# Two projection loads between an exchange's copies, four output stores from GpSimd to SyncE, and two broadcast loads behind an exchange, in a fused cross-attention block

## The chip, the core and the metric

The kernel runs on one core of one Trainium2 chip. The metric is device time in microseconds (us); the kernel before the change has a median of 761.75 us over three runs (761.52 to 764.06).

A core has five engines, each with a queue of its own that is worked off in order: TensorE (PE in the profile, with PEld for its weight loads), VectorE (DVE), ScalarE (ACT), GpSimd (POOL) and SyncE (SP), which here only issues DMA transfers. Engines wait for each other through semaphores. An SPq row of the profile is SP's queue at a transfer's issue, not the transfer itself.

## What is computed

One cross-attention block over 4 batches, 512 queries and 512 keys, width 512, 16 heads of 32, float32 throughout. The mask is all true.

```python
x = layer_norm(hidden, ln1_w, ln1_b)
q = x @ q_w + q_b
k = enc @ k_w + k_b
v = enc @ v_w + v_b                            # each split into 16 heads of 32
attn = softmax(where(mask, q @ k.T / sqrt(32), lowest))
hidden = (attn @ v) @ cproj_w + cproj_b + hidden
y = gelu(layer_norm(hidden, ln2_w, ln2_b) @ fc_w + fc_b)   # 512 -> 2048
out = hidden + y @ proj_w + proj_b                         # 2048 -> 512
```

## The kernel before

**Blocks.** Attention is cut into 32 blocks, numbered p = 0 to 31. Block p treats batch p // 8, a group of four heads (w = p // 2, so four groups a batch) and half of the queries (half = p % 2). `block` (L349) computes eight tiles of scores on PE (L329); VectorE adds the mask and takes the minimum (L335), ScalarE exponentiates (L339), and VectorE transposes the probabilities in 32 x 32 squares into a buffer `tb` (L347, L372), of which there are two, used in turn. PSUM tiles for scores and products come from two rings of four, used in order (`acc_tile`).

**The exchange.** The transposed squares must then move between the four groups of 32 partitions. `copies` (L397) does it: four GpSimd copies stay within a group (L405), and twelve DMA copies on SP of 136 KB each (L410) go from one group to another, in three rounds d = 1, 2, 3 of four. The target is a tile `pT`, or for some blocks a part of the big buffers `gt` and `xe`. `attend(w, half)` (L413), the product of probabilities and values (L427), reads the whole target some blocks later: in the order written out near the end, block p begins with `attend` of block p - 2 from p = 10 on, and of p - 3 from 3 to 8.

**The order of work.** There is no scheduler. `put(p, ...)` lists for each block the work that fills PE between its scores and its end: preparation of later heads' q, k, v, the output product of the attention, and of the MLP a pair of `fc` blocks (`fc_by_pair`, PE L668) or parts of the projection (`proj`, L774 and L755). `fill(0)` and `fill(1)` run items up to a cost of `CHAIN`, the exchange is issued after `fill(1)`, and `fill(2)` runs what is left. A cost of 0.0 lets an item run within the same `fill`; `next_` gives 0.01, so that an item behind a full `fill(1)` goes to `fill(2)`, behind the exchange.

**MLP weights.** Eight slots in `pbt` take turns (`load_mlp`, L604): a load of 256 KB is issued from SP, in the order of `weights`, as soon as in the program's order the last use of its slot has been issued. Batch 0's projection works on blocks of sums and differences in place, so its slots are also read by late adds on GpSimd (`join`, L622), which block 29 pops from `S["late"]`. Block 29 does the last part of batch 0's projection and the `fc` pair 2 of batch 1; block 30 does pair 3 and the first product of batch 1's projection (`proj_whole`, L755), which reads the four weights 2, 3, 0, 1 in that order. Weights 2 and 3 are loaded in block 28's wake, 0 and 1 by `load_mlp` after block 29's exchange, with two more behind them.

**Batch 0's result** (`hid4`) is complete after those late adds. `store_out(0)` (L828) writes it with four DMA stores of 256 KB, issued from GpSimd at L830. Block 30 then loads two tiles of batch 1 into the same buffer (`load_hid`, L555), which waits for the stores of those tiles, and GpSimd adds a row to them (L438).

**Batch 1's first normalisation.** Its row factors are stored to DRAM and read back, broadcast to 128 partitions, by two loads of 256 KB into `hid2` (`load_rn`, L216). GpSimd multiplies and adds them to the four transposed input tiles `raw` (`ln1_rows`, L221, four operations in block 2 and four in block 3), and ScalarE applies weight and bias (`ln1_affine`, L225, block 4). In block 1 the loads are issued together with batch 1's encoder input (`load_enc`, 1 MB), ahead of that block's exchange.

After block 31, the rest of the MLP runs in larger pieces (`last_mlps`, L668, L901 and others).

Of the kernel before, what the change touches and what calls it, by code (L numbers as in the profile page):

```python
# [20 lines left out]
P = 128  # L21
# [32 lines left out]
def xattn_block(ctx: ExitStack, tc: tile.TileContext, x, rawT, encT, mask, q_w, k_w, v_w, c_w, fc_w, p_w, vecs, rows, out):  # L54
    nc = tc.nc
# [40 lines left out]
    def k_q(w, i):  # L96
        n = w % 4 * 2 + i
        return pbt[:, n * D : (n + 1) * D]

    def mlp_w(n):  # L100
        return pbt[:, (n + MW) * D : (n + MW + 1) * D]
# [16 lines left out]
    S = {"gelu": [], "late": []}  # L118
    count = [0, 0, 0, 0, 0, 0]
    Q = [nc.sync]  # L120

    def acc_tile(name):
        n = count[5]
        count[5] += len(banks) > 1
        return banks[n // 4 % len(banks)].tile([P, D], F32, tag="acc", name=name)
# [51 lines left out]
    def queue(b):  # L177
        return Q[0] if b else nc.sync

    def load_enc(b):  # L180
        for d in range(ND):
            queue(b).dma_start(out=eT[:, d, :], in_=encT[b, ts(d, P), :])
# [17 lines left out]
    def load_raw(b):  # L200
        S["xn", b] = [tiles.tile([P, L], F32, tag="xn", name=f"raw_{b}_{d}") for d in range(ND)]
        for d in range(ND):
            nc.sync.dma_start(out=S["xn", b][d], in_=rawT[b, ts(d, P), :])

    def store_rn(b):
        nc.vector.transpose(rnT, rn)
        d = S["rn", b] = dram.tile([2, L], F32, tag=f"rn{b}", name=f"rn{b}")
        for i in range(NI):
            nc.sync.dma_start(
                out=d.rearrange("a (t i q) -> i (a t) q", i=NI, q=HD)[i], in_=rnT[i * HD : i * HD + 2 * NT, :]  # L210
            )

    def load_rn(b):
        S["rows", b] = [hid2[:, i] for i in range(2)]
        for i in range(2):
            nc.sync.dma_start(out=S["rows", b][i], in_=S["rn", b][i : i + 1, :].broadcast_to([P, L]))  # L216

    def ln1_rows(b, *ds):
        for d in ds:
            for i, op in enumerate((ALU.mult, ALU.add)):  # L220
                nc.gpsimd.tensor_tensor(S["xn", b][d], S["xn", b][d], S["rows", b][i], op)  # L221
# [21 lines left out]
    def load_w(w, queue=None, names=("wk", "wq", "wv")):  # L243

        if w >= NW:
            return
        g = w % NG
        for i, (n, src) in enumerate((("wk", k_w), ("wq", q_w), ("wv", v_w))):
            if n in names:
                S[n, w] = kqv_w(w, i)  # L250
                (queue or Q[0]).dma_start(out=S[n, w], in_=src[:, g, :, :])

    def next_w(w, name):
        if w != SINGLE - 1:
            load_w(w + (2 if w < SINGLE else 1), names=(name,))
# [11 lines left out]
    def prep_q(w):  # L267
        b, g = divmod(w, NG)
        qT = k_q(w, 1)
        parts = [slice(0, L)] if w else [slice(0, 2 * P), slice(2 * P, L)]  # L270
        for c in parts:
            acc = acc_tile(f"accq_{w}_{c.start}")[:, c]
            for d in range(ND):
                nc.tensor.matmul(acc, S["wq", w][:, d, :], xT[:, d, c], start=(d == 0), stop=(d == ND - 1))  # L274
            nc.scalar.activation(qT[:, c], acc, AF.Identity, bias=qb[:, g : g + 1], scale=-scale)
        next_w(w, "wq")
        S["qT", w] = qT

    def prep_v(w):
        b = w // NG  # L280
        v = five.tile([P, NT, P], F32, tag="v", name=f"v_{w}")
        acc = acc_tile(f"accv_{w}")
        for t in range(NT):
            for d in range(ND):
                nc.tensor.matmul(  # L285
                    acc[:, ts(t, P)], eT[:, d, ts(t, P)], S["wv", w][:, d, :],
                    start=(d == 0), stop=(d == ND - 1),
                )
        load_w(w + 2, names=("wv",))
        nc.scalar.copy(v, acc.rearrange("p (t f) -> p t f", t=NT))  # L290
        S["v", w] = v
        if w:
            v_bias(w)
# [25 lines left out]
    def v_bias(w):  # L319
        v, bias = S["v", w], row[:, 2, ts(w % NG, P)]  # L320
        nc.gpsimd.tensor_tensor(v, v, bias[:, None, :].broadcast_to([P, NT, P]), ALU.add)  # L321
# [59 lines left out]
            exchange()  # L381
        fill(2)

    waiting, held = [], {}

    def target(w, half):
        pair = 2 * w + half
        return "gt" if pair in IN_G else "xe" if pair in IN_XE else "pT"
# [8 lines left out]
    def copies(w, half):  # L397
        tb, to = S["tb", w, half], target(w, half)
        if to == "pT":
            pT = one.tile([P, NI, PW + 2 * HD], F32, tag="pT", name=f"pT_{w}_{half}")  # L400
        else:
            pT = (gt if to == "gt" else xe).rearrange("p (i n) -> p i n", i=NI)

        for i in range(NI):
            nc.gpsimd.tensor_copy(pT[ts(i, HD), i], tb[ts(i, HD), i])  # L405
        for d in range(1, NI):
            for i in (0, 2, 1, 3):
                j = (i + d) % NI

                nc.sync.dma_start(out=pT[ts(j, HD), i], in_=tb[ts(i, HD), j])  # L410
        S["pT", w, half] = pT

    def attend(w, half):  # L413
# [175 lines left out]
    for name, b, i, *_ in products:  # L589
# [6 lines left out]
    weights = [(*k, n, i % MW) for i, (k, n) in enumerate(last_use.items())]  # L596
# [3 lines left out]
    free = [  # L600
        next((o[3] for o in reversed(weights[:i]) if o[4] == w[4]), -1) for i, w in enumerate(weights)
    ]

    def load_mlp():  # L604

        while count[0] < len(weights) and free[count[0]] < count[1]:
            name, b, f, _, n = weights[count[0]]
            w = mlp_w(n)
            if name == "fc":
                w = w.rearrange("p (d f) -> p d f", d=ND)  # L610
            Q[0].dma_start(out=w, in_=fc_w[:, f, :, :] if name == "fc" else p_w[ts(f, P), :])
            S[name + "w", b, f] = w if name == "fc" else n + MW
            count[0] += 1
# [10 lines left out]
    def a_sums(a11, a12, a21, a22, s1, s2, s3, s4, engine=None):  # L624
        add(engine or nc.vector, s1, a21, a22)
        sub(s3, a11, a21, engine)
        sub(s2, s1, a11, engine)
        sub(s4, a12, s2, engine)
# [69 lines left out]
    def raw_pair(b, c):  # L698
        return [S["fcw", b, 2 * c + i] for i in range(2)]

    def fc_sums(ahead=2):

        while count[3] < len(fc_pairs) and count[3] < count[4] + ahead:
            b, c = fc_pairs[count[3]]
            if ("fcw", b, 2 * c + 1) not in S:
                return
            x, y = raw_pair(b, c)
            s = wsum[:, count[3] % 2]
            a_sums(x[:, :2], x[:, 2:], y[:, :2], y[:, 2:], s[:, 0], s[:, 1], y[:, :2], s[:, 2], nc.gpsimd)
            if b == 0:  # L710
                nc.gpsimd.dma_start(out=sums_dram[c, :, :3], in_=s)
                nc.gpsimd.dma_start(out=sums_dram[c, :, 3], in_=y[:, :2])
            S["ws", b, c] = s[:, 0], s[:, 1], y[:, :2], s[:, 2]
            count[3] += 1
# [48 lines left out]
    def proj(b, q, part):  # L763
# [61 lines left out]
        if (q, part) != (NQ - 1, 2):  # L825
            load_mlp()

    def store_out(b):  # L828
        for t in range(NT):
            nc.gpsimd.dma_start(out=out[b, ts(t, P), :], in_=S["hid", b, t])  # L830

    wa = [gt[:, i * 2048 : i * 2048 + 1024].rearrange("p (i d f) -> p i d f", i=2, d=ND) for i in range(2)]
    ws = [gt[:, i * 2048 + 1024 : i * 2048 + 2048].rearrange("p (i k f) -> p i k f", i=4, k=2) for i in range(2)]
# [264 lines left out]
    CHAIN, TURN = 3.4, 0.5  # L1098

    def do(fn):  # L1100
        return [(0.0, fn)]

    def next_(fn):
        return [(0.01, fn)]

    def A(w):
        if w >= NW:
            return []
        return [
            (CHAIN, lambda: prep_k(w)),  # L1110
            (CHAIN, lambda: prep_q(w)),
            (CHAIN, lambda: prep_v(w)),
        ]
# [69 lines left out]
    def some(n):  # L1183
        taken = []
        while n > 0:
            n -= 1 if mlp[0][0] == CHAIN else 2
            taken.append(mlp.pop(0))
        assert n == 0
        return taken
# [4 lines left out]
    def hid_(b, *ts_):  # L1194
        return do(lambda: load_hid(b, ts_))
# [21 lines left out]
    def put(p, *work, before=(), mid=()):  # L1217

        work = [item for part in work for item in part]
        ahead[p], mids[p] = list(before), list(mid)  # L1220
        fills[p] = work

    k2, q2, v2 = A(2)
    k3, q3, v3 = A(3)
# [1 line left out]
    k5, q5, v5 = A(5)  # L1226
    k6, q6, v6 = A(6)
    put(0, [(CHAIN, lambda: prep_v(1)), v2], do(lambda: (load_raw(1), store_rn(1))), [k2])
    put(1, [k3, (0.0, lambda: prep_q(1)), (CHAIN, lambda: (prep_v(3), load_enc(1), load_rn(1)))])
    put(2, [q2], [q3], do(lambda: ln1_rows(1, 0, 1)))  # L1230
    put(3, [k4], do(lambda: ln1_rows(1, 2, 3)), [v4])
    put(4, [k5, v5], do(lambda: ln1_affine(1)))
# [39 lines left out]
    put(26, c[3:], do(lambda: attend(12, 0)), pre(0, 3, "w"), some(1))  # L1272
    put(27, some(3))
    put(28, some(3))
    put(29, some(1), do(lambda: (fc_sums(), S["late"].pop()())), some(2), do(lambda: (load_mlp(), store_out(0))))
    put(30, some(3), mid=hid_(1, 2, 3))
    put(31, some(3))

# [2 lines left out]
    for p in range(2 * NW):  # L1281
        w, half = divmod(p, 2)
# [81 lines left out]
```

## Time and profile before

| what | value |
|---|---|
| median of three runs | 761.75 us (761.52 to 764.06) |
| the profiled execution's own time | 762.13 us |
| its span, from the first to the last instruction | 760.4 us |
| mean granted PE clock over the span | 0.997 |
| DMA, mean over the span | 177 GB/s |
| SP's transfers (queue q1) | 126.73 MB |
| GpSimd's transfers (queue q0) | 7.01 MB |

A row of a timeline gives start and length in us, engine, line, operation, and output and input by their names; behind it stands in brackets how long the engine was idle before, and for whom it waited. A row of the chain gives start, length and who held the end at that time. In a table of stages the busy time of each engine is followed by the granted PE clock, the busy share of the 16 DMA engines and GB/s. Lines are those of the kernel before; behind the change they are two or three higher.

### The profile page before, as it was taken

How to read it: one execution, taken by the hardware profiler on the slowest of the kernel's cores; microseconds unless marked ns; L12 is line 12 of the kernel's file. 1: busy time of each engine (PE TensorE's matmuls, PEld its weight loads, DVE VectorE, ACT ScalarE, POOL GpSimd, SP SyncE). 2: the span in 40 equal slices, each digit the busy share in tenths (PEclk: the TensorE clock that was granted, in tenths of full speed). 3: DMA queues.
4: the chain of work that ended last, by engine and by line, in shares of the span. 5: the costliest groups of instructions: out<-in, count | busy, mean ns of one | idle time of the engine just before them, and what ended most of it. 6: DMA issues, size and time to landing. Idle time of an engine off the chain costs nothing.

```text
span 760.4 us, 13322 instructions
## 1 busy us (share of the span) xinstructions
PE 751.2 (99%) x4514; PEld 535.9 (70%) x4514; DVE 618.2 (81%) x1229; ACT 341.0 (45%) x776; POOL 405.6 (53%) x405
## 2 busy tenths in 40 slices
PE   8999999999999999999999999999999999999998
PEld 6655555467667546576655775458888889988998
DVE  3888999879988779877988998848877986957765
ACT  2566776555874575648843577401202221021200
POOL 1539448368687987667869975532050005403153
PEclk9999999999999999999999999999999999999999
DMA  9999888466796797666747758667824512046001
GB/s 324 341 248 245 208 215 251 107 191 185 212 253 208 199 267 188 166 187 165 196 117 213 178 144 250 152 203 236 270 98 134 156 37 91 29 139 220 2 15 43
DMA packets 60580, 134.62 MB, mean 177 GB/s; under 512 B 11312, under 2 KB 17072, under 8 KB 60384
## 3 DMA queue, kind: packets, MB, share of 16 engines
q1 hardware_dynamic: 58448, 126.73, 59.0%
q0 software_dynamic: 1920, 7.01, 2.8%
q8 instruction: 36, 0.59, 0.3%
q14 instruction: 32, 0.26, 0.1%
q10 hardware_dynamic: 144, 0.02, 0.0%
HBM read 69.23 MB, written 11.02 MB: 106 GB/s over the span
## 4 chain that ended last, share of the span: by engine, by line
PE 93%; DMA 2%; POOL 2%; DVE 1%; SPq 1%; issue 0%; DVEq 0%; POOLq 0%
PE q L668 23%; PE r L901 10%; PE sc L329 8%; PE av L427 7%; PE acck L262 7%; PE accq L274 7%; PE accc L469 6%; PE accv L285 5%; PE accp L755 4%; PE accv L310 3%; PE q1p L962 2%; PE tp L169 1%; SPq L410 1%; PE q1j L774 1%; PE q2j L774 1%; PE q7j L774 1%
## 5 line engine op out<-in xcount | busy, mean ns | idle before, releaser
L339 ACT ACTIVATE ptt<-ptt,mn 128x512 f32<-128x512 f32 x256 | 181.7, 711 | 146.9 <-DVE mn L335 146.9
L335 DVE CUSTOM_DVE_ANT_0 ptt<-sc,mb 128x512 f32<-128x512 f32 x256 | 160.6, 682 | 19.5 <-PE sc L329 19.5
L347 DVE STREAM_TRANSPOSE tb<-ptt 128x1024 f32<-128x1024 f32 x128 | 153.3, 1217 | 1.5 <-ACT ptt L339 1.5
L405 POOL COPY pT<-tb 32x1088 f32<-32x1088 f32 x96 | 104.6, 1089 | 34.7 <-DVE oT L432 11.8
L668 PE MATMUL q<-yT,gt 128*128 128x256 f32 x320 | 78.9, 379 | 0.0
L689 ACT ACTIVATE ga<-ga,vec 128x512 f32<-128x512 f32 x40 | 26.7, 714 | 93.3 <-DVE ga L622 83.6
L329 PE MATMUL sc<-pbt 32*128 32x512 f32 x512 | 67.1, 615 | 0.0
L668 PEld LDWEIGHTS q<-yT,gt 128*128 128x128 f32 x320 | 60.7, 190 | 8.2
L668 PE MATMUL q<-ys,gt 128*128 128x256 f32 x240 | 61.6, 379 | 0.0
L262 PE MATMUL acck<-xe,ptt 128*128 128x512 f32 x128 | 58.7, 601 | 0.0
L274 PE MATMUL accq<-xe,ptt 128*128 128x512 f32 (+1 forms) x136 | 58.1, 573 | 0.0
L668 PEld LDWEIGHTS q<-ys,gt 128*128 128x128 f32 x240 | 45.6, 190 | 6.2
L622 DVE TENSOR_TENSOR ga<-q,ga 128x512 f32<-128x512 f32 (+1 forms) x60 | 36.2, 603 | 15.6 <-PE q L668 12.6
L427 PE MATMUL av<-pT,v 128*32 128x256 f32 x768 | 46.4, 382 | 1.9 <-POOL gt L619 1.9
L339 ACT ACTIVATION_READ_ACCUMULATOR ptt<-ptt,mn 128x1 f32 x256 | 47.8, 187 | 0.0
L274 PEld LDWEIGHTS accq<-xe,ptt 128*128 128x128 f32 x136 | 25.0, 190 | 30.4 <-issue 23.0
L438 POOL TENSOR_TENSOR hid<-hid,row 128x512 f32<-128x512 f32 x18 | 23.9, 1356 | 41.6 <-DMA hid<-xa 41.6
L329 PEld LDWEIGHTS sc<-pbt 32*128 32x128 f32 x512 | 27.7, 183 | 26.0 <-issue 17.5
L262 PEld LDWEIGHTS acck<-xe,ptt 128*128 128x128 f32 x128 | 23.0, 190 | 31.4 <-issue 21.5
L469 PE MATMUL accc<-wc,oT 128*128 128x512 f32 x96 | 42.5, 597 | 0.0
L321 POOL TENSOR_TENSOR v<-v,row 128x512 f32<-128x512 f32 x16 | 20.3, 1278 | 40.6 <-ACT v L290 29.8
L285 PEld LDWEIGHTS accv<-ptt,xe 128*128 128x128 f32 x320 | 36.9, 192 | 5.8 <-DVE mn L335 2.5
(264 smaller groups left out, 1440.8 us busy)
## 6 DMA issues: line engine op xcount, KB each, us to landing
pT<-tb SPq DMA_DIRECT2D x288, 136.0 KB
pbt<-p_w_dram SPq DMA_DIRECT2D x40, 256.0 KB
gt<-ws SPq DMA_DIRECT2D x20, 512.0 KB
gt<-tb SPq DMA_DIRECT2D x48, 136.0 KB
xe<-tb SPq DMA_DIRECT2D x48, 136.0 KB
pbt<-fc_w_dram SPq DMA_DIRECT2D x24, 256.0 KB
gt<-fc_w_dram SPq DMA_DIRECT2D x20, 256.0 KB
ptt<-k_w_dram SPq DMA_DIRECT2D x16, 256.0 KB
```

The costliest lines, as they stand in the source:

```text
L262: nc.tensor.matmul(acc, S["wk", w][:, d, :], eT[:, d, :], start=(d == 0), stop=(d == ND - 1))
L274: nc.tensor.matmul(acc, S["wq", w][:, d, :], xT[:, d, c], start=(d == 0), stop=(d == ND - 1))
L285: nc.tensor.matmul(acc[:, ts(t, P)], eT[:, d, ts(t, P)], S["wv", w][:, d, :], start=(d == 0), stop=(d == ND - 1),)
L329: nc.tensor.matmul(S["sc", w, qt][h], qT[r, ts(qt, P)], kT[r, :], start=True, stop=True)
L335: nc.vector.tensor_tensor_reduce(out=s, in0=S["sc", w, qt][h], in1=S["mb", w // NG], scale=1.0, scalar=FMAX, op0=ALU.add, op1=ALU.min, acc ...
L339: nc.scalar.activation(s, s, AF.Exp, bias=mn, scale=-1.0, accum_out=S["sums", w][:, qt, h : h + 1])
L347: nc.vector.transpose(tv[:, qt % 2, 2 * k : 2 * k + 2], S["ps", w, qt, k])
L405: nc.gpsimd.tensor_copy(pT[ts(i, HD), i], tb[ts(i, HD), i])
L427: nc.tensor.matmul(av[ts(h, HD), : 2 * P].rearrange(shape, **kw), v[:, t, ts(h, HD)], p[t][h], start=(t == 0), stop=(t == NT - 1),)
L469: nc.tensor.matmul(acc, S["oT", b][:, g, ts(t, P)], wc[:, g, :], start=(g == 0), stop=(g == NG - 1))
L668: nc.tensor.matmul(o, x[:, k], y[:, k], start=(k == 0), stop=(k == 1))
L901: nc.tensor.matmul(r, x[:, c], w[:, c], start=(c == 0), stop=(c == NP // 2 - 1))
```

## The change

Three edits:

1. The first two of the four projection loads that followed block 29's exchange (weights 0 and 1) are issued on SP between that exchange's first round of four copies and the other eight. `copies` gets a hook for it (`between`), and `load_mlp` a limit on the number of loads. The other two loads stay behind.
2. Batch 0's four output stores are issued by SP, behind block 29's exchange and ahead of the remaining two loads; before, GpSimd issued them, and the loads stood ahead in the program.
3. The two broadcast loads of batch 1's row factors go from ahead of block 1's exchange to behind it, still on SP.

On SP the order around block 29 is, before: 12 copies, 4 projection loads, 2 reloads of `hid`, 2 projection loads. After: 4 copies, 2 projection loads, 8 copies, 4 stores, 2 projection loads, 2 reloads, 2 projection loads. The first moved load waits for the second of GpSimd's late adds. PE's, VectorE's and ScalarE's instructions and their order are the same; GpSimd loses its four stores.

```diff
-    waiting, held = [], {}
+    waiting, held, between = [], {}, {}
...
                 nc.sync.dma_start(out=pT[ts(j, HD), i], in_=tb[ts(i, HD), j])
+            if d == 1:
+                between.pop((w, half), lambda: None)()
...
-    def load_mlp():
+    def load_mlp(most=len(weights)):
 
-        while count[0] < len(weights) and free[count[0]] < count[1]:
+        end = min(count[0] + most, len(weights))
+        while count[0] < end and free[count[0]] < count[1]:
...
     def store_out(b):
         for t in range(NT):
-            nc.gpsimd.dma_start(out=out[b, ts(t, P), :], in_=S["hid", b, t])
+            nc.sync.dma_start(out=out[b, ts(t, P), :], in_=S["hid", b, t])
...
-    put(1, [k3, (0.0, lambda: prep_q(1)), (CHAIN, lambda: (prep_v(3), load_enc(1), load_rn(1)))])
+    put(1, [k3, (0.0, lambda: prep_q(1)), (CHAIN, lambda: (prep_v(3), load_enc(1)))], next_(lambda: load_rn(1)))
...
-    put(29, some(1), do(lambda: (fc_sums(), S["late"].pop()())), some(2), do(lambda: (load_mlp(), store_out(0))))
+    put(29, some(1), do(lambda: (fc_sums(), S["late"].pop()())), some(2), do(lambda: (store_out(0), load_mlp())))
+    between[14, 1] = lambda: load_mlp(2)
```

## Prediction

> **What bounds the kernel now.** I read the page's busy times first, then TensorE's waits, then the timeline of the one long wait that this change can reach.
>
> ```profile
> PE 751.2 (99%) x4514; PEld 535.9 (70%) x4514; DVE 618.2 (81%) x1229; ACT 341.0 (45%) x776; POOL 405.6 (53%) x405
> ```
>
> ```profile
> PE av L427 <- POOL gt L619: 1.9, 1, 1.9
> PE accp L755 <- DMA pbt<-p_w_dram: 1.7, 1, 1.7
> ```
>
> TensorE (PE) is busy for 99% of the span. No matmul is added or removed, so the change can only win where PE stands still or runs slowly, and lose by making PE wait anew. Two waits over a microsecond remain inside the work; the second, at L755 for a projection load, is the one that the moved loads end.
>
> ```profile
> 467.15 1.88 PE L755 MATMUL accp<-pbt,gt 128*128 128x512 f32 x4
> 470.75 3.01 PE L755 MATMUL accp<-pbt,gt 128*128 128x512 f32 x4 [1.73 <-DMA pbt<-p_w_dram]
> 473.69 2.80 PE L427 MATMUL av<-xe,v 128*32 128x256 f32 x32
> 476.42 1.14 PE L329 MATMUL sc<-pbt 32*128 32x512 f32 x8
> ```
>
> ```profile
> 476.49 1.93 PE sc L329 x16
> 478.42 10.50 PE accp L755 x24
> 488.92 1.86 PE av L427 x32
> ```
>
> ```profile
> 466.00:478.00 12.00, 10.27 (x63) 4.24 (x61) 8.06 (x16) 6.09 (x10) 4.04 (x4) 0.86 1.00 310
> 473.00:474.00 1.00, 1.00 (x5) 0.20 (x8) 0.20 (x1) 0.36 (x1) 0.08 (x1) 0.50 0.71 266
> 217.00:226.00 9.00, 7.12 (x64) 4.57 (x63) 6.31 (x16) 6.07 (x10) 7.47 (x7) 1.00 1.02 315
> ```
>
> The first fence is PE's timeline (start, length), the second the chain, the third the stage table (after the busy times: granted PE clock, DMA share, GB/s). In block 30 the eight matmuls of one projection product begin at 467.15, stop in the middle for two weights, and the attention product and block 31's scores follow at 473.69 and 476.42: 476.42 - 467.15 = 9.27 us. The same work undisturbed stands a little later: three projection products in 10.50, so 3.50 each, and an attention product in 1.86, together 5.36. **The disturbance costs 9.27 - 5.36 = 3.91 us**, over twice the 1.7 that the table of waits shows. The clock column says why: 0.86 of full speed over these 12 us, a loss of 0.14 x 12 = 1.68 us, with 0.50 just after the wait. So 1.68 is slow clock and the remaining 2.23 is waiting.
>
> **Part by part: the two loads.** Who delays them is on SyncE (SP) and GpSimd (POOL):
>
> ```profile
> 450.91 0.90 SPq L611 DMA_DIRECT2D pbt<-p_w_dram  x2
> 456.30 8.38 SPq L410 DMA_DIRECT2D xe<-tb  x12
> 464.77 3.81 SPq L611 DMA_DIRECT2D pbt<-p_w_dram  x4
> 470.24 1.40 SPq L555 DMA_DIRECT2D hid<-xa  x2
> 471.73 0.86 SPq L611 DMA_DIRECT2D pbt<-p_w_dram  x2
> 472.68 7.66 SPq L410 DMA_DIRECT2D pT<-tb  x12
> ```
>
> ```profile
> 461.30 1.47 SPq L410
> ...
> 464.77 5.93 DMA pbt<-p_w_dram
> ```
>
> ```profile
> 456.53 2.52 POOL L622 TENSOR_TENSOR hid<-pbt,hid 128x512 f32<-128x512 f32 x2
> 458.99 4.47 POOL L405 COPY xe<-tb 32x1088 f32<-32x1088 f32 x4
> 463.40 2.16 POOL L830 DMA_DIRECT2D out_dram<-hid  x4
> 473.92 2.50 POOL L438 TENSOR_TENSOR hid<-hid,row 128x512 f32<-128x512 f32 x2 [8.35 <-DMA hid<-xa]
> 476.36 4.47 POOL L405 COPY pT<-tb 32x1088 f32<-32x1088 f32 x4
> ```
>
> ```profile
> DMA to landing us min/median/max: 2.8/5.5/6.2
> ```
>
> These are SP's timeline, two rows of the chain, POOL's timeline, and the landing times of POOL's four stores. Before, the load that PE waits for is issued at 464.77, behind the twelve copies, and lands 5.93 us later. After, it stands behind four copies. One copy holds the issue row for 1.47; the other eleven take (8.38 - 1.47)/11 = 0.63 each, so four end at 456.30 + 4 x 0.63 = 458.8. The load overwrites a slot that POOL's late adds read until 456.53 + 2.52 = 459.05; SP waits 0.25 there and issues both in 0.90 (row at 450.91), by 460.0. Their landing is bounded by the 5.93 above and, as the highest in these rows, 6.98 for block 1's broadcast rows (below): 467.0 at worst. PE needs them after half of a product, at 467.15 + 1.75 = 468.9. The wait is gone at either bound: 2.23 us. The slow clock began after the wait, so I take it to go too: 1.68 more.
>
> What is late next? First the **eight copies** behind the two loads: from 460.0, 8 x 0.63 and once more the slow one (1.47 - 0.63 = 0.84) give a last issue at 465.9 instead of 464.7. The attention product that reads them now starts at 467.15 + 3.50 = 470.65. By 5.93 they land at 471.8, a stall of 1.2; by the stores' shortest, 2.8, at 468.7, none. I take none: the 5.93 was seen behind a full exchange and beside POOL's stores, which now come after the copies. Second, **VectorE (DVE)**:
>
> ```profile
> 470.82 1.94 DVE L622 TENSOR_TENSOR gt<-q,gt 128x512 f32<-128x512 f32 x3
> 473.80 0.69 DVE L759 TENSOR_TENSOR hid<-accp,hid 128x512 f32<-128x512 f32 x1 [1.03 <-PE accp L755]
> 476.63 0.42 DVE L432 TENSOR_TENSOR oT<-av,xe 128x256 f32<-128x256 f32 x1 [2.14 <-DMA pbt<-p_w_dram]
> 477.58 0.69 DVE L335 CUSTOM_DVE_ANT_0 ptt<-sc,mb 128x512 f32<-128x512 f32 x1 [0.53 <-PE sc L329]
> ```
>
> DVE's adds of block 30 end at 472.76 whatever PE does. Then follow 0.69 and 0.42, and block 31's first score is read by 472.76 + 0.69 + 0.42 + 0.69 = 474.56. PE, whose eight PSUM tiles go round, needs that tile again after its scores: 467.15 + 5.36 + 1.93 = 474.44. Loss: 0.1. DVE's idle 1.03 + 2.14 + 0.53 is what it gives up, and from there it keeps pace.
>
> **The stores on SP.** POOL loses 2.16 us of issuing, which nobody waits for: it then stands idle 8.35 us for the reloaded rows. SP gains four issues, 1.8 by the row of 0.90 for two, from 465.9 to 467.7; two more loads, whose weights are for later products, follow by 468.6. The reload of `hid` (L555) has to wait for the last two stores, as before: that let the two reloads go at 470.24 and at the latest by 470.24 + 1.40 = 471.6. After, by 2.8 to 6.2 from issue, the last lands between 470.5 and 473.9. Then come two loads and block 30's twelve copies (0.86 + 7.66), needed by the attention product that now starts at 488.92 - 3.8 = 485.1. I take landing near 471, the old time, since the queue moves over 300 GB/s here (310 above) and the stores' 1 MB, sent from 466 on, needs 3.4 us: cost nothing, and the copies end about where they did, 480.3. The worst bound is a rival below.
>
> **Block 1's rows.** The two broadcast loads now follow twelve copies:
>
> ```profile
> 49.39 1.08 SPq L216 DMA_DIRECT2D hid<-rn  x2
> 50.58 9.85 SPq L410 DMA_DIRECT2D gt<-tb  x12
> ```
>
> ```profile
> 56.37 5.22 POOL L221 TENSOR_TENSOR raw<-raw,hid 128x512 f32<-128x512 f32 x4 [2.84 <-DMA hid<-rn]
> 61.54 4.47 POOL L405 COPY pT<-tb 32x1088 f32<-32x1088 f32 x4
> ```
>
> ```profile
> 74.43 2.37 DVE L347 STREAM_TRANSPOSE tb<-ptt 128x1024 f32<-128x1024 f32 x2
> ```
>
> ```profile
> 80.19 2.94 ACT L225 ACTIVATE xe<-raw,vec 128x512 f32<-128x512 f32 x4
> ```
>
> ```profile
> 476.00:756.00 280.00, 279.98 (x1639) 241.59 (x1631) 214.88 (x358) 49.68 (x100) 81.12 (x72) 1.00 0.39 122
> ```
>
> The loads took 56.37 - 49.39 = 6.98 to release POOL. After, they are issued from about 49.4 + 9.85 = 59.3 and release it between 62.1 (2.8) and 66.3 (6.98). Behind POOL's four row operations (5.22) stands block 2's copy (4.47), whose source buffer DVE's transposes at 74.43 overwrite: copied by 71.8 to 76.0, so nothing up to a DVE delay of 1.6. I take 63, POOL done at 72.7, cost 0, because the loads' 6.98 was behind a megabyte of other loads. ACT's affine at 80.19 needs another four operations: 63 + 5.22 + 4.47 + 5.22 = 77.9, in time. No PE wait stood at block 1, so the earlier copies win nothing.
>
> **Sum.** 2.23 + 1.68 - 0.1 = 3.8 us. From 476 to 756 PE is busy 279.98 of 280 us, so the gain is carried to the end. The profiled execution took 762.13 (span 760.4, 1.7 around it); 762.13 - 3.8 = 758.3. It lies 0.38 over the median 761.75, so in the measure of the medians I forecast **757.9**.
>
> **The rivals.**
>
> *The slow clock stays* (or is not usual in the timed runs): then only the 2.23 - 0.1 go, 761.75 - 2.1 = 759.6.
>
> ```profile
> 220.28 1.07 PE L427 MATMUL av<-pT,v 128*32 128x256 f32 x16 [1.88 <-POOL gt L619]
> ```
>
> For it: this wait at L427, PE's other long one, is as long as the projection's 1.73, and in its stage (217 to 226, quoted above) the clock is 1.00. Against: the drop stands right behind the disturbance, where PE waited twice within 5 us, for 2.23 in all. The Trainium skill (TensorE: Matmul & The Clock Gate, "HAM oscillation — how this bites in real kernels") asks for PE gaps above about 3.4 us before the clock halves, by which this gap would not have caused the drop and 2.1 would be gained instead of 3.8. The trace shows 0.50 right behind a gap of 1.73, so the measurement decides against the rule here.
>
> *Block 29's copies land late*: the 1.2 us above, 757.9 + 1.2 = 759.1. Against it, stores no longer move beside them.
>
> *Slower: the stores hold SP.* If the last store lands only at 473.9, then half of 1.40, 0.86 and 7.66 put block 30's last copy at 483.1, and with 5.93 it lands at 489.0 against 485.1: PE stalls 3.9 in that attention product, and a slow-clock stretch like the present one adds 1.68. 757.9 + 5.6 = 763.5, slower than now. It takes both upper ends; it decides from a stall of 3.8 - 1.7 = 2.1 on.
>
> *It doesn't do what it says*: POOL's late adds slip and SP stands at the moved load, all copies behind it; the wait is exchanged for another of its size, 761.7. Against: these adds end at 459.05 and nothing ahead of them changes.
>
> **How the numbers follow.** Forecast case 0.72 (757.4 to 758.4, its middle at the bound), slow clock stays 0.11, late copies 0.05, stores hold SP 0.05, does nothing 0.03, something unseen and slower 0.04. 757.2 to 760.0 takes in the first three, trimmed at their edges: about 8 in 10. About 0.5% (3.8 us, 757.94) is what a measurement of this kernel can tell from no change. The forecast case lies half on each side, so faster 0.36; the other half, the next four cases but a hundredth: same 0.59; slower 0.05.
>
> **What would show it.** Right: no PE wait for `p_w` at L755; the L555-to-L410 rows of SP near their old times; clock 1.00 all through block 30; block 31's scores 3.8 us earlier; POOL's row operations at about 63 with DVE's transposes of block 4 still at 74.4. Wrong: a PE wait at L427 in blocks 30 or 31, a new clock drop at the wait of 220.28, or a DVE gap ahead of the transposes at 74.4.

## The result, and the profile after

| | before | after |
|---|---|---|
| median of six runs each | 761.57 us (759.66 to 764.06) | 756.87 us (755.90 to 758.21) |
| ratio, with its 95% interval | | 0.9943 (0.9921 to 0.9964) |
| the profiled execution's own time, and its span | 762.13, 760.4 | 758.21, 756.4 |

The change gains 0.57%, 4.70 us in the medians. The forecast of 757.9 lies inside the interval (0.9921 to 0.9964 of 761.57 is 755.6 to 758.8), but the median lies 0.3 under the lower end of the range, 757.2. The forecast was made from a median of 761.75; the ratio on that base gives 757.4, inside the range. The two profiled executions differ by 762.13 - 758.21 = 3.92, which is what the sum of 3.8 was made for. That agreement is partly luck. PE's last matmul ends 4.60 earlier (756.75 and 752.15), and the stores behind it take 0.6 longer (3.65 and 4.25; in all the profiles here 3.6 to 4.3); and the 4.60 is made up of other pieces than the sum named.

PE's busy time, and PE's waits in the whole span, of the kernel after (engine, line, tile, whom it waited for; us in total, times, longest):

```profile
PE 748.7 (99%) x4514; PEld 536.2 (71%) x4514; DVE 617.6 (82%) x1229; ACT 341.0 (45%) x776; POOL 403.6 (53%) x401
```

```profile
PE av L429 <- POOL gt L622: 1.9, 1, 1.9
PE warm L1157 <- POOL ident masks.py:199: 1.3, 1, 1.3
PE av L429 <- POOL raw L221: 0.2, 1, 0.2
```

The wait for a projection load is gone from the list, and the new one of 0.2 stands at 259.2, far from all three edits. PE's timeline in block 30, and the stages that the prediction quoted, after:

```profile
466.09 3.60 PE L758 MATMUL accp<-pbt,gt 128*128 128x512 f32 x8
469.61 1.93 PE L429 MATMUL av<-xe,v 128*32 128x256 f32 x32
471.48 2.34 PE L329 MATMUL sc<-pbt 32*128 32x512 f32 x16
473.75 2.84 PE L758 MATMUL accp<-pbt,gt 128*128 128x512 f32 x6
```

```profile
466.00:478.00 12.00, 12.00 (x68) 5.43 (x67) 11.76 (x26) 10.27 (x22) 5.98 (x6) 1.00 0.93 286
472.00:752.00 280.00, 279.98 (x1632) 242.07 (x1624) 214.98 (x361) 50.00 (x101) 82.63 (x73) 1.00 0.39 124
217.00:226.00 9.00, 7.14 (x64) 4.76 (x64) 6.33 (x18) 6.11 (x13) 7.46 (x7) 1.00 1.00 314
```

From the product's start to block 31's scores it is 471.48 - 466.09 = 5.39, where 9.27 was before and 5.36 was forecast: 3.88 saved, the wait and the slow clock together (the clock column reads 1.00, before 0.86). The scores then take 2.34 instead of 2.00, so 3.54 remain. (The last row, the stage of PE's other long wait, is unchanged: 1.9 us of waiting, and the clock at 1.00.) But the product itself begins at 466.09, and before it began at 467.15. **Another 1.06 us was won ahead of the stage that the prediction looked at.** The matching rows of VectorE (DVE) and PE show where, first before, then after:

```profile
64.29 2.37 DVE L347 STREAM_TRANSPOSE tb<-ptt 128x1024 f32<-128x1024 f32 x2 [1.50 <-ACT ptt L339]
```

```profile
68.87 3.15 PE L329 MATMUL sc<-pbt 32*128 32x512 f32 x16
71.96 3.27 PE L262 MATMUL acck<-xe,ptt 128*128 128x512 f32 x7
```

```profile
62.65 2.37 DVE L347 STREAM_TRANSPOSE tb<-ptt 128x1024 f32<-128x1024 f32 x2
```

```profile
68.81 2.00 PE L329 MATMUL sc<-pbt 32*128 32x512 f32 x16
70.74 3.70 PE L262 MATMUL acck<-xe,ptt 128*128 128x512 f32 x8
```

Block 4's scores took 3.15 before and 2.00 after, and the next product starts 1.22 earlier. VectorE had been idle for 1.50 ahead of block 3's transposes. They overwrite the buffer `tb` that block 1's twelve copies read. By the completion events of the trace, the last of these copies landed at 64.01 (fifteen of its sixteen completion events stood by 62.42), and the transposes began 0.28 later; after the change this copy was issued 2.1 earlier and landed at 61.37, and they began as soon as VectorE was free. The row puts the idle time down to ScalarE's `ptt` (L339), but the four tiles that these transposes read were ready by 62.7. PE's waiting doesn't appear as waiting at all: the sixteen matmuls are strung out and all counted as busy. The Trainium skill (Perfetto Trace Analysis, "Identifying the Most-Contended Engine") says that the busy share of the matmuls is no good measure of how close a kernel is to the limit, since pipelined instructions look smaller in the trace. The two rows agree that the busy share misleads, though here it errs the other way: one busy group holds 1.15 us of waiting.

SP around the two places, after. The two loads are issued at 458.03 to 458.86 (forecast: by 460.0), the stores behind the last copy at 464.39, and the queue closes up behind them.

```profile
455.24 2.42 SPq L410 DMA_DIRECT2D xe<-tb  x4
458.03 0.83 SPq L614 DMA_DIRECT2D pbt<-p_w_dram  x2
458.91 5.43 SPq L410 DMA_DIRECT2D xe<-tb  x8
464.39 2.15 SPq L833 DMA_DIRECT2D out_dram<-hid  x4
466.64 1.36 SPq L614 DMA_DIRECT2D pbt<-p_w_dram  x2
468.38 1.31 SPq L557 DMA_DIRECT2D hid<-xa  x2
469.79 0.86 SPq L614 DMA_DIRECT2D pbt<-p_w_dram  x2
470.70 9.26 SPq L410 DMA_DIRECT2D pT<-tb  x12
```

```profile
49.39 8.92 SPq L410 DMA_DIRECT2D gt<-tb  x12
58.35 1.07 SPq L216 DMA_DIRECT2D hid<-rn  x2
```

```profile
62.26 1.28 POOL L221 TENSOR_TENSOR raw<-raw,hid 128x512 f32<-128x512 f32 x1 [8.78 <-DMA hid<-rn]
64.89 3.88 POOL L221 TENSOR_TENSOR raw<-raw,hid 128x512 f32<-128x512 f32 x3 [1.35 <-DMA hid<-rn]
68.70 4.47 POOL L405 COPY pT<-tb 32x1088 f32<-32x1088 f32 x4
```

```profile
73.72 2.37 DVE L347 STREAM_TRANSPOSE tb<-ptt 128x1024 f32<-128x1024 f32 x2
```

Block 1's copies begin where the rows had stood. GpSimd (POOL) gets its rows at 62.26 and 64.89, copies by 73.17, and block 4's transposes start at 73.72 with VectorE not idle ahead of them: this side of the step held.

### The profile page after: what moved, and what is told of

Read it like the earlier page. It is cut to its first block, busy times and chain, and to the rows that moved or that the text cites. A ratio compares the mean times of both kernels' runs of the same rounds, so it can differ in the third digit from the quotient of the medians.

```text
span 756.4 us, 13322 instructions
## 1 busy us (share of the span) xinstructions
PE 748.7 (99%) x4514; PEld 536.2 (71%) x4514; DVE 617.6 (82%) x1229; ACT 341.0 (45%) x776; POOL 403.6 (53%) x401
## 4 chain that ended last, share of the span: by engine, by line
PE 95%; POOL 3%; DMA 1%; issue 0%; SPq 0%; DVE 0%; DVEq 0%; POOLq 0%
PE q L671 24%; PE r L904 10%; PE sc L329 8%; PE av L429 7%; PE acck L262 7%; PE accq L274 7%; PE accc L471 6%; PE accv L285 5%; PE accp L758 4%; PE accv L310 3%; PE q1p L965 2%; PE tp L169 1%; POOL pT L405 1%; PE q3j L777 1%; PE q1j L777 1%; PE q7j L777 1%
## 5 line engine op out<-in xcount | busy, mean ns | idle before, releaser
L339 ACT ACTIVATE ptt<-ptt,mn 128x512 f32<-128x512 f32 x256 | 181.7, 711 | 142.3 <-DVE mn L335 142.3
L671 PE MATMUL q<-ys,gt 128*128 128x256 f32 x240 | 61.6, 379 | 0.0
L429 PE MATMUL av<-pT,v 128*32 128x256 f32 x768 | 46.4, 382 | 2.1 <-POOL gt L622 1.9
L339 ACT ACTIVATION_READ_ACCUMULATOR ptt<-ptt,mn 128x1 f32 x256 | 47.8, 187 | 0.0
```

The costliest lines, as they stand in the source:

```text
L339: nc.scalar.activation(s, s, AF.Exp, bias=mn, scale=-1.0, accum_out=S["sums", w][:, qt, h : h + 1])
L429: nc.tensor.matmul(av[ts(h, HD), : 2 * P].rearrange(shape, **kw), v[:, t, ts(h, HD)], p[t][h], start=(t == 0), stop=(t == NT - 1),)
L671: nc.tensor.matmul(o, x[:, k], y[:, k], start=(k == 0), stop=(k == 1))
```

## The experiments

**The theories.** A: two gains, the loads in block 30 (3.5 us) and the rows at block 3's transposes (1.1 us). Rival B, the prediction as written: all of it in block 30, worth 3.8. After the first four kernels came C: the parts work together, since time won at block 3 is lost again if the loads are late; D: only the loads count. Beside them stood the question why the loads were late, and what lowers the clock.

The kernels were run in three sets of four, each set on a chip of its own (here X, Y and Z) together with the kernel before. "Lost clock" counts the timed executions whose mean granted clock over the span is 0.998 or lower: half speed for 3.4 us, as in the profile of before, is 1.7 us of 757, or 0.002. The count is rough: one execution of the changed kernel at 0.998 took 756.96, no longer than its others. The wait is PE's wait for a projection load in the profiled execution.

| kernel | chip | median, us | ratio (95%) | wait, us | lost clock |
|---|---|---|---|---|---|
| before | X | 759.15 | | | 10 of 35 |
| loads only (e1) | X | 757.65 | 0.9971 (0.9953 to 0.9989) | 0 | 0 of 12 |
| stores only (e2) | X | 759.61 | 1.0007 (0.9985 to 1.0029) | 1.76 | 7 of 12 |
| rows only (e3) | X | 760.01 | 1.0011 (0.9992 to 1.0029) | 3.04 | 5 of 12 |
| all three, loads last (e4) | X | 757.15 | 0.9969 (0.9952 to 0.9985) | 0 | 0 of 12 |
| before | Y | 760.97 | | | 23 of 32 |
| all three (e5) | Y | 756.28 | 0.9941 (0.9920 to 0.9962) | 0 | 0 of 10 |
| loads and rows (e6) | Y | 757.36 | 0.9943 (0.9925 to 0.9961) | 0 | 0 of 11 |
| wait filled (e7) | Y | 758.93 | 0.9981 (0.9961 to 1.0000) | 1.24 | 0 of 12 |
| stores twice (e8) | Y | 763.20 | 1.0022 (1.0003 to 1.0040) | 3.78 | 11 of 12 |
| before | Z | 761.05 | | | 19 of 35 |
| loads and stores (e9) | Z | 757.39 | 0.9956 (0.9942 to 0.9971) | 0 | 0 of 12 |
| all three (e10) | Z | 757.44 | 0.9960 (0.9942 to 0.9978) | 0 | 1 of 12 |
| order only (e11) | Z | 757.38 | 0.9948 (0.9928 to 0.9968) | 0 | 0 of 12 |
| loads only (e12) | Z | 757.98 | 0.9967 (0.9946 to 0.9989) | 0 | 2 of 12 |

### Which part carries the gain

**Loads only (e1):** before, with the hook and `between[14, 1] = lambda: load_mlp(2)`; stores on GpSimd, rows in their old place.

```diff
+            if d == 1:
+                between.pop((w, half), lambda: None)()
...
+    between[14, 1] = lambda: load_mlp(2)
```

> Before, with the first edit alone: two projection loads between block 29's copies; the stores stay on GpSimd and the broadcast rows ahead of block 1's exchange. Theory A (two gains): the gain is made in two places, about 3.5 us in block 30 by the loads (3.88 of wait and slow clock, 0.35 given back to VectorE) and about 1.1 us at block 4's scores by the third edit. It expects 761.6 - 3.5 = 758.1 us, no PE wait for a projection load in block 30, and block 4's scores (the sixteen matmuls at about 68.8) still in 3.15 us. Theory B (the prediction as written: all of the gain is in block 30, the rest of the 4.7 is scatter of the start): the start of block 4's scores and their 3.15 us change as chance has it, and the time comes to about the changed kernel's own, 757 us. A slow clock that was rare in the timed runs of the kernel before would leave only the wait's 2.1: 759.5.

Measured 757.65, half a microsecond under what A expected, but on a chip where before itself takes 759.15, so the gain is 0.29%, 2.2 us, and not 3.5. Block 4's scores took 2.00, although the rows stood in their old place; of that below. A new wait stands in block 30, for block 29's last copies:

```profile
465.02 3.60 PE L758 MATMUL accp<-pbt,gt 128*128 128x512 f32 x8
468.95 1.93 PE L429 MATMUL av<-xe,v 128*32 128x256 f32 x32 [0.33 <-DMA xe<-tb]
470.81 2.00 PE L329 MATMUL sc<-pbt 32*128 32x512 f32 x16
```

With 0.33 of wait the scores take 2.00 and not 2.34: the late copies give VectorE the time that it needs, so the two small losses don't add. A's 3.5 took the slow clock for granted; on this chip 10 of 35 executions of before lost clock, so most of them had only the wait to win back, which the expectation puts at 2.1.

**Stores only (e2):** `nc.gpsimd` to `nc.sync` in `store_out`, and `(store_out(0), load_mlp())` in block 29.

> Before, with the second edit alone: batch 0's four stores on SyncE, in the order stores first and the four projection loads behind them. The loads that PE waits for in block 30 are then issued behind twelve copies and four stores. Theory A: by the changed kernel's row of 2.15 us for the four stores, the loads go out 2.1 us later, the wait of 1.73 becomes about 3.9, and the time 761.6 + 2.1 = 763.7 us; block 4's scores keep their 3.15. Rival (stores on GpSimd were what delayed the load, so taking them away speeds its landing): the wait stays at 1.7 or less and the time is 761.6 or lower. If the clock drop grows with the wait, 764.5 or more.

The wait did not grow to 3.9, it stayed at 1.76, and the time is that of before. The expected sum forgot that the stores, on either queue, were ahead of the loads already.

**Rows only (e3):** `load_rn(1)` from `put(1, ...)`'s first list to `next_(lambda: load_rn(1))`.

> Before, with the third edit alone: the two broadcast rows behind block 1's exchange. Theory A: block 1's copies end 2 us earlier on SyncE, VectorE's transposes of block 3 no longer wait (idle 1.50 before, 0 after), block 4's scores take 2.00 instead of 3.15, and PE keeps about 0.9 to 1.15 of it to the end: 761.6 - 1.1 = 760.5 us, while block 30 keeps its wait of 1.7 and its clock of about 0.5 for 3.4 us. Theory B (the prediction: the third edit is worth nothing): 761.6 us, and block 4's scores take 3.15 us or change without the edit's doing.

A's local part came true: VectorE isn't idle at block 3, and block 4's scores take 2.00. But the time is that of before. The lead over the stores-only kernel of the same chip is 1.18 us at the product behind block 4's scores and 0.05 at 279 us. There it is taken back by a wait hidden in the same way, inside a group of scores, which the stores-only kernel doesn't have (2.00). VectorE was late again, but by another cause: it waited for GpSimd, 1.77 us here and 0.54 in the stores-only kernel, and both then started within 0.1 us of each other:

```profile
276.00 3.21 PE L329 MATMUL sc<-pbt 32*128 32x512 f32 x16
279.14 2.41 PE L274 MATMUL accq<-xe,ptt 128*128 128x512 f32 x5
```

```profile
277.01 0.69 DVE L470 TENSOR_TENSOR h<-accc,h 128x512 f32<-128x512 f32 x1 [1.77 <-POOL h L438]
```

And in block 30 this execution waited 3.04 for the load, the second place that could swallow a lead.

**All three (e5) and loads with rows (e6),** the changed kernel itself, and with its stores back on GpSimd behind `load_mlp()`.

> The changed kernel itself once more, all three edits, to be compared with its parts on one chip. The runs so far on that chip gave ratios to before of 0.9971 for the loads alone, 1.0007 for the stores alone and 1.0011 for the rows alone. Theory C (the parts work together: before has two hidden losses in a row, VectorE's wait at block 3 and the loads' late landing in block 30, and time won at the first is lost again at the second unless the loads are early): 0.9955, about 755.8 where before takes 759.2, with no execution at a mean clock of 0.998 or lower. Theory D (only the loads count): the loads' own 0.997, about 757.

> The changed kernel with the stores left on GpSimd: the first and the third edit. Theory C expects all of the gain without the stores: 0.9955 of before, block 4's scores in 2.00 us, no PE wait for a projection load in block 30, and perhaps 0.3 us of wait at block 30's attention product for the last copies, as with the loads alone. If the stores on SyncE are needed (they keep the last eight copies clear of other transfers), the wait is 0.3 to 1.2 us and the ratio 0.997.

0.9941 repeats the first result on chip Y. The ratio alone would speak for C, but chip Y isn't chip X: there 23 of 32 executions of before lost clock. Without the stores' move the ratio is the same within the intervals, though the median is 1.08 higher, and 0.53 us of wait for the copies takes the place of VectorE's 0.34.

**Loads and stores (e9), all three (e10), loads only (e12),** on one chip. e9 is the changed kernel with `load_rn(1)` back in its old place; e12 is e1.

> The first and second edit without the third: the broadcast rows are back ahead of block 1's exchange. To be set against all three edits on the same chip. Theory C (the rows' gain counts once the loads are early): block 3's transposes wait up to 2 us for the last copy of block 1, block 4's scores take up to 3.8 us instead of 2.00, and the time is 0.5 to 1.1 us over that of all three. Theory D (only the loads count; later waits take the rows' gain back): the same time as all three within 0.4 us, although the wait at block 3 is there.

> All three edits, as the yardstick of the other kernels on this chip. By the two results so far (0.9943 and 0.9941) 0.994 where most executions of before lose clock in block 30, and about 0.997 on a chip where most of them do not; its own time 756 to 757.2 either way, with no wait for a projection load and no clock under 0.999.

> The first edit alone again, on the same chip as the other three. Theory: the stores' move is worth nothing that shows, since the loads alone leave a wait of 0.3 to 0.5 us for block 29's last copies where the stores on SyncE leave 0.34 us for VectorE; so the same time as the loads with the stores, within 0.4 us. Rival (stores on GpSimd beside the last copies cost what the prediction's bound of 1.2 us says): 0.8 to 1.2 us more.

757.39, 757.44, 757.98: D's forecast, no difference that twelve executions show. Two expectations were missed by a little: all three edits lie 0.24 over their 757.2, and the loads alone lie 0.59 over the loads with the stores, between the 0.4 of the theory and the 0.8 of its rival. The wait at block 3 was there in e9 (scores of 3.36) and cost its profiled execution 1.36 us at that place against e10's 2.00, and at the end of PE's work it is 1.7 behind; the rest is scatter (at 259 us e9 waits 0.85, at 305 us e10 waits 0.35, both for other things). In the eight profiles with the rows in their old place block 4's scores took 3.15, 2.86, 3.47, 3.76, 3.36 (before, e2, e7, e8, e9) and three times 2.00 (e1, e11, e12); in all six with the rows behind the exchange they took 2.00. The landing of block 1's last copy goes with it: 60.6 to 61.6 in those six, 61.5 to 62.8 in the three, 63.4 to 64.1 in the five that waited. So the third edit does remove a wait, one that comes in five executions of eight. What it is worth in the median is between nothing and about 1 us, and these runs don't say more.

### Why the load came late

**All three, loads last (e4):** `if d == 1:` becomes `if d == 3:`, so the two loads follow all twelve copies and stay ahead of the stores.

> The changed kernel, with the two projection loads behind all twelve copies of block 29's exchange instead of behind four (stores still on SyncE behind them, rows still behind block 1's exchange). The place of the loads alone is undone. Theory A: the load is issued at about 463.5 instead of 458.9, PE waits again about 1.7 us in block 30 with the clock at about 0.5 for some 3.4 us behind it, and the time is 756.9 + 3.5 = 760.4 us. Rival (the stores beside the copies, not the place, made the load late): it lands by 468 although it is issued last, PE waits under 0.5 us, the clock stays at 1.00, and the time is 757.0 to 757.5.

The rival won: no wait at all, 757.15. **Order only (e11):** no hook, rows in their old place; stores on SP, and in block 29 `(load_mlp(2), store_out(0), load_mlp())`.

> The smallest edit that the theory of the queue asks for: stores on SyncE, and behind the whole exchange of block 29 the two awaited loads first, then the four stores, then the other two loads. Nothing between the copies, rows ahead of block 1's exchange. Theory (what counts is that the two loads are ahead of the megabyte of stores): the loads land 2.8 to 3.3 us after issue, PE waits at most 0.5 us for them, the clock holds, and the time is that of the loads with the stores (first kernel of this call) within 0.3 us. Rival (the place between the copies is needed, and the loads-last kernel was saved by PE coming later): a wait of 1 us or more, and 1 to 3 us over it.

Again no wait, and 757.38 beside 757.39 of loads and stores. SP and PE of this kernel:

```profile
452.58 8.86 SPq L410 DMA_DIRECT2D xe<-tb  x12
461.54 1.02 SPq L612 DMA_DIRECT2D pbt<-p_w_dram  x2
462.62 2.24 SPq L831 DMA_DIRECT2D out_dram<-hid  x4
464.96 1.41 SPq L612 DMA_DIRECT2D pbt<-p_w_dram  x2
```

```profile
463.43 3.60 PE L756 MATMUL accp<-pbt,gt 128*128 128x512 f32 x8
```

The first load is issued at 461.54, and PE runs through its second half from 463.43 + 1.75 = 465.2 without a stop: the load took under 3.7 us, and by its completion event 2.81. The rows-only kernel issues the same load behind the same twelve copies, but behind GpSimd's stores. Its chain and GpSimd's timeline:

```profile
462.64 6.69 DMA pbt<-p_w_dram
```

```profile
460.86 2.17 POOL L830 DMA_DIRECT2D out_dram<-hid  x4
```

6.69 instead of 2.81. Before, it was 5.93, with the stores issued from 463.40 and the load at 464.77. So the load was late because a megabyte of stores stood ahead of it, and the copies ahead of it cost only their issue. By an estimate from the 2.81, before's own load would have landed at 464.77 + 2.81 = 467.6, ahead of PE's need at 468.9. What was not run is the loads behind all twelve copies and ahead of stores that stay on GpSimd.

**Stores twice (e8):** the stores-only kernel with `(store_out(0), store_out(0), load_mlp())`; each store is made twice, with the same data.

> The stores alone on SyncE ahead of the four projection loads, as before, and each of the four stored twice with the same data: a megabyte more ahead of the loads. Four stores took 2.06 us to issue and 2.4 us from the first landing to the last. Theory (the load is late by what stands ahead of it in the queue): PE's wait of 1.76 becomes 3.9 to 4.5 us, the ratio goes from 1.0007 to 1.004 by the wait alone; if a longer wait drops the clock more often (5 to 7 of 12 at waits of 1.8 to 3.0), all or nearly all of the executions drop and the ratio is about 1.006. Rival (the load's landing time is set by its own size and the other loads): the wait stays under 2.5 us.

```profile
461.99 5.01 SPq L830 DMA_DIRECT2D out_dram<-hid  x8
467.05 2.33 SPq L611 DMA_DIRECT2D pbt<-p_w_dram  x4
```

```profile
470.54 1.98 PE L755 MATMUL accp<-pbt,gt 128*128 128x512 f32 x4 [3.78 <-DMA pbt<-p_w_dram]
```

Another megabyte ahead, another 2.0 us of wait, as the theory had it (3.78, forecast 3.9 to 4.5). The ratio, 1.0022, stays under the 1.004 to 1.006 that was expected; on this chip before itself mostly lost clock. On one queue the delay is in the issue (467.05 instead of 464.34; the landing takes 3.44 and 3.74): SP stands at the stores. On two queues it is in the landing. Either way the load is late with the stores ahead of it.

### What lowers the clock

**Wait filled (e7):** the kernel before, with two extra matmuls ahead of the product that waits. They use its first weight and write into the same tile, which the product's own start overwrites.

```diff
+        for _ in range(2 * ((b, q, t) == (SPLIT, 0, 0))):
+            n = S["pw", b, FQ // 2]
+            nc.tensor.matmul(acc, gT[0][:, FQ // 2, ts(t, P)], pbt[:, n * D : (n + 1) * D], start=True, stop=True)
```

> The kernel before, with two extra matmuls of the first weight and the first tile ahead of the projection product that waits; their sums are overwritten by the product's own start, so the result is unchanged. They take 2 x 0.88 = 1.75 us of the 1.73 of wait. Theory (idling is what lowers the clock): the wait at the projection load falls to 0 to 1.3 us, no execution has a mean clock of 0.998 or lower (10 of 35 of before did), and the time is that of before's undropped executions, about 758.5 where before's median is 759.2. Rival (the drop comes from something else at that place, such as transfers): 3 or 4 of 12 executions still drop and the median is 759.2 or, where the wait is shorter than the two matmuls, up to 760.

```profile
465.45 1.88 PE L754 MATMUL accp<-pbt,gt 128*128 128x512 f32 x4
467.17 1.88 PE L758 MATMUL accp<-pbt,gt 128*128 128x512 f32 x4
470.29 1.98 PE L758 MATMUL accp<-pbt,gt 128*128 128x512 f32 x4 [1.24 <-DMA pbt<-p_w_dram]
```

In this execution PE would have waited 3.0; with 1.7 of it filled, 1.24 were left. None of twelve executions lost clock, where 23 of 32 of before did on the same chip, with the same transfers at the same place. Idling lowers the clock, and not the traffic. The time, 758.93, is that of before's own executions without the loss (median 759.11 on chip Y). With waits of 1.8, 3.0 and 3.8 in their profiled executions the loss came in 7, 5 and 11 of 12 (e2, e3, e8). But the length alone doesn't decide: before lost clock at 1.73, and the profiled execution of e8 waited 3.78 and lost none; its stage around the wait, with the clock at 1.00:

```profile
466.00:478.00 12.00, 8.22 (x58) 3.32 (x57) 7.91 (x19) 6.52 (x13) 3.35 (x3) 1.00 1.02 325
```

## Why the prediction was right, and where it was not

- **The wait for the load goes** (2.23): right in all nine profiles of kernels that issue the two loads ahead of the stores. The working had the wrong cause. It put the load's lateness to its place "behind the twelve copies" and took four copies instead of twelve as the cure. e4 and e11 leave it behind all twelve and lose nothing; what had to be passed were the stores. Against only those executions of before that lost no clock (758.75, 759.11 and 759.69 on X, Y and Z), the medians of the kernels with the loads early lie 1.1 to 2.8 lower, around the 2.1 that this term less VectorE's lag was to bring. The prediction used this very effect further on, when it costed the eight later copies at nothing because the stores "now come after the copies".
- **The slow clock goes with it** (1.68): right in its cause (e7), and in its size in the profiled execution (half speed for 3.4 us is 1.7). The rival "or is not usual in the timed runs" was half true: 52 of 102 executions of before lost clock. The median of those lies 2.3, 2.2 and 2.8 us over the others' on the three chips, more than 1.68; whether these executions also wait longer isn't known. So this term is a chance of about one half, with 3 in 10 on chip X and 7 in 10 on chip Y, and the gain follows it: 0.9969 for e4 on X, 0.9941 for e5 on Y. One profiled execution can't show that.
- **VectorE's lag** was put at 0.1 and measured 0.34 (scores of 2.34). The prediction looked at the wrong tile. It took the next projection product to wait for the tile of the first scores, but that product starts 0.52 behind the last matmul of the scores in all fourteen profiles, whether they were delayed or not. What waits is the last tile of the scores: eight tiles in turn make it the one that the attention product has just filled, and VectorE frees that with its multiplication at L434, which ended at 472.64:

```profile
472.23 0.41 DVE L434 TENSOR_TENSOR oT<-av,xe 128x256 f32<-128x256 f32 x1
```

In this profile the last tile's first matmul starts at 472.69, 1.22 behind the start of the scores; it is the same in all six profiles whose scores take 2.33 or 2.34, by the trace's single records. L434 ends 1.16 behind that start. In the other eight it ends 0.61 to 0.76 behind it, and the matmul starts at 0.98. The prediction's own times would have given it: L434 ends at 472.76 + 0.69 + 0.42 = 473.87, and the tile is wanted at 467.15 + 5.36 + 0.98 = 473.49, a loss of 0.38.

- **The eight later copies cost nothing**: right where the stores follow on SP; with the stores on GpSimd they cost a wait of 0.33, 0.53 and 0.41 (e1, e6, e12), well inside the bound of 1.2, and VectorE's lag falls away in return.
- **The stores on SP cost nothing**: right. The reloads go out by 468.38 + 1.31 = 469.7 (forecast: 471.6 at the latest), block 30's copies end at 470.70 + 9.26 = 479.96, forecast 480.3, and the attention product that reads them doesn't wait. Whether they gain anything isn't settled: the ratios are 0.9941 beside 0.9943 without them on chip Y and 0.9956 beside 0.9967 on chip Z, within their intervals, but the medians lie 1.08 and 0.59 lower with them, both the same way.
- **Block 1's rows**: the step that failed is "No PE wait stood at block 1, so the earlier copies win nothing". The table of waits had no such row, but the copies held block 3's transposes, and through them block 4's scores, by 1.2 in the profiled execution. What the step feared, the later rows, cost nothing as argued.
- **The gain is carried to the end**: right from block 30 on (279.98 of 280 busy). It didn't hold for the gain made at block 4, of which the rows-only kernel shows that it can be lost on the way.
- **The range** ended at 757.2 because it allowed for nothing ahead of block 30. Besides the 1.1 at block 4, the wait of 1.9 at L429 (before L427, at 220.28) that both first profiles show, and that the prediction took as fixed, is in none of the twelve others. Why it comes and goes isn't known. That the forecast still came within about 1 us is in part luck: the sum counted the clock's term in full, which about half of the executions pay, and put the rows' gain at block 4 at nothing, and the two errors have opposite signs.

## What to carry to other kernels

When a load comes late, look first at what moves the most bytes ahead of it, on every queue, and not at the nearest instructions ahead of it on its own: two loads of 256 KB put ahead of 1 MB of stores brought all of the gain here that twelve executions can show, by their order on one queue (e11, with the stores on SP too). Look for hidden waits by comparing a group with its like: the same sixteen matmuls in 3.15 and in 2.00 say more than PE's busy share. When tiles are used in turn, ask for every tile who frees it, and not for the first alone. And before a price is taken from one execution's clock, ask how many executions pay it.

## What was not expected of the hardware

- The clock loss is a matter of chance at the same place of the same kernel: 10 of 35, 23 of 32 and 19 of 35 executions of before on three chips, and 4 of 99 of the changed kernel and the others that have the loads early. The Trainium skill (TensorE: Matmul & The Clock Gate, "What's actually happening") says that PE's activity is measured in a free-running window of about 3.4 us. A window whose place is not tied to the program would fall differently in each execution, and the loss of 3.4 us in the profile of before agrees with its length; that was not tested by itself. The Trainium skill's rule that only gaps above about 3.4 us matter (same page, "HAM oscillation — how this bites in real kernels") doesn't agree: 0.50 behind a gap of 1.73, and 1.00 behind one of 3.78.
- A 256 KB load landed 2.8 us after its issue with only copies ahead of it, and 5.9 to 6.7 us after it with a megabyte of stores just ahead on another engine's queue.
